# One adaLN transformer block with a routed expert layer on one core: one activation table for logarithm and exponential, the second norm in steps of a block, and four operations placed elsewhere

## The chip, the core and the metric

The kernel runs on one core of one Trainium2 chip. The core has a matrix engine, TensorE (PE in the profile; its weight loads are listed as PEld), and three engines for elementwise work: VectorE (DVE), ScalarE (ACT) and GpSimd (POOL). SyncE (SP) issues most of the transfers (DMA), POOL the gathers and scatters. Each engine works through its own queue in the order in which the program was written, and waits for the others by semaphores. PE multiplies from the on-chip memory SBUF and writes its products into eight banks of PSUM, which the other engines read out.

The metric is the time of one execution on the device in microseconds (us), and lower is better. All arithmetic is in float32.

## The reference

x holds 4 batches of 512 tokens with 512 features. A conditioning vector c makes six rows of modulation a batch. The block is, cut to what matters:

```python
mod = (silu(c) @ wmod).reshape(4, 6, 1, 512)
sa, ca, ga, sb, cb, gb = mod[:, 0], ..., mod[:, 5]      # ga, gb kept away from zero
h = layernorm(x) * (1 + ca) + sa
x = x + ga * attention(h)        # 16 heads of 128, causal softmax, Wq Wk Wv Wo with biases
h = layernorm(x) * (1 + cb) + sb
x = x + gb * ffn(h)
# ffn: softmax router over 8 experts, the best 2 of them a token (silu(h Wg) * (h Wu)) Wd
#      of width 352, weighted and summed, plus a shared expert of width 704
# layernorm: (x - mean) / sqrt(var + 1e-5), over the 512 features
```

## The kernel before

**Products by seven.** Every large product is cut into 2 by 2 blocks and made with seven block products in place of eight (`seven`, L515). The operands therefore carry seven slots: four blocks as they are, and sums of them, made by `sums_of_a` (L490) and `sums_of_b` (L497) into slots 4, 5 and 6 and, in place, into slot 2 or 1. `PROD` (L487) says which two slots each product takes. PE makes them in the order 1, 2, 6, 7, 5, 4, 3: the first two take the blocks as loaded (slots 0, and 1 with 2), the third takes slot 5 of both sides, the fourth slots 2 and 4, the fifth slots 4 and 1, the sixth 3 and 6, the seventh 6 and 3. A product lies in a PSUM bank of the tag "w", of which there are three, until DVE or ACT has read it out. `most_of_b` (L504) and `rest_of_b` (L510) are `sums_of_b` in two pieces: slots 4, 5 and 6 first, without touching slot 1, and then slot 1 in place.

**Opening (L869 to L884, L1061 to L1073).** SP loads c, the modulation weights wm for SA, x of batch 0, wm for CA, the biases, and then the weights wk, wq and wv, whose sums POOL makes as they land. `normed` (L211) takes the first norm: for each of the four blocks of 128 tokens, statistics on DVE (L227, L228), then rstd as exp(-0.5 ln(var + eps)) with Ln and Exp on ACT (L233, L234), then the scaling on DVE (L244). `modulate` (L166) makes one row set of modulation on PE. `quadrants` (L878) turns the normed x by PE transposes (`turned_block`, L267; `turn`, L275), applies the modulation and makes the sums.

**Attention (loop from L1076).** The heads go in 16 groups, G, of four heads, u; four groups a batch. For each head, `scores` (L782 to L800) makes four rows of logits, their masked maxima (DVE), Exp (ACT), and the scaling by the reciprocal of the sums (rsum, L797, on DVE, then L800 on ACT). `attend` (L803) transposes the weights on PE (L810), copies them out as probT (L818 on DVE, L820 on ACT) and multiplies with v (po, L824). `weave_at` writes the steps of these generators into the queues by hand: after each step of attention so many steps of the next projections (`fill`), and at the positions in `spots` one step of a side generator. The side generators are the first norm and the turning of the next batch, and `second_norm` (L949) of the batch before: `normed` with n = 2, which also multiplies by ga, adds x (L221, L222), and applies rows cb and sb (L261 on DVE, L262 on POOL), and then the router (`route`, L293), whose first step transposes the normed blocks. `fine` lists the blocks after which `normed` ends a step; its default, (1,), puts two blocks into a step. All queues but POOL's follow the written order exactly.

**Shared expert, first half (L1579 to L1614).** For batches 0 and 1, the turned second-norm outputs h2s are loaded; `tail_products` (L1210) multiplies the last 64 columns of the shared expert, `shared_tail` (L1223) applies Silu, and `sums_of_b` makes the sums of h2s, for batch 0 on POOL and for batch 1 on DVE. `shared(0)` (PE lines L1241 and L1322) then runs its products, while `slots_found` does the second norm and the routing of batch 3 beside it (here the scaling is on ACT, L253, and `idle` is true). The tiles' weights and rows are loaded during the last products.

**Expert tiles (L1616 to L1647).** 36 tiles of 128 routed tokens: `tile_in` (L1452) transposes a tile's rows and copies them to xT, `tile_hidden` makes gate and up (pgt and put, L1468), `tile_down` the result yt, which `keep` stores (L1507). A branch for more than 36 tiles follows (L1649). Pools of SBUF are opened for one phase each (`open_phase`): "tiles" takes the place of "half1", "half2" the place of "tiles", and a tile in the new pool has to wait until the last reader of that place is done.

**Shared expert, second half (from L1659).** The same for batches 2 and 3, with the gathering of the experts' results.

Of the kernel before, what the change touches and what calls it, by code (L numbers as in the profile page):

```python
# [44 lines left out]
EPS = 1e-5  # L45
SA, CA, GA, SB, CB, GB = range(6)
# [3 lines left out]
def adaln_block_kernel(  # L50
# [105 lines left out]
    nc.scalar.activation(cs, cT, AF.Silu)  # L156
# [9 lines left out]
    def modulate(sec, wm):  # L166
        pm = bank("ps", f"pm_{sec}")[:B, :]
        for c in range(NC):
            nc.tensor.matmul(
                pm, lhsT=cs[:, c, :], rhs=wm[:, c, :], start=(c == 0), stop=(c == NC - 1)  # L170
            )
        row = work.tile([B, D], F32, tag="gy", name=f"row_{sec}")
# [12 lines left out]
        if sec in (SA, CA):  # L185
            pt = bank("pt", f"pmt_{sec}")
            for c in range(NC):
                nc.tensor.transpose(
                    pt[:, c * B : (c + 1) * B], row[:, c * P : (c + 1) * P], ident[:B, :B]
                )  # L190
            nc.vector.tensor_copy(
                mod[:, sec].rearrange("p c b -> p (c b)"), pt[:, : NC * B]
            )
        else:
            nc.sync.dma_start(out=mod_rows[sec], in_=row)
# [13 lines left out]


    def normed(b, n, fine=(1,)):  # L211


        if n == 1:
            src = xh = late["first"]
        else:
            src = xres[b]
            xh = late["x"]
            rows = late["mod"]
            for t in range(NTB):  # L220
                nc.vector.tensor_mul(src[:, t, :], src[:, t, :], ga_bc)  # L221
                nc.gpsimd.tensor_add(src[:, t, :], src[:, t, :], xh[:, t, :])  # L222
                yield
        mv = small.tile([P, NTB, 2], F32, tag="mv", name=f"mv_{n}_{b}")
# [7 lines left out]
        nc.vector.tensor_scalar_add(rstd, mv[:, :, 1], EPS)  # L232
        nc.scalar.activation(rstd, rstd, AF.Ln)  # L233
        nc.scalar.activation(rstd, rstd, AF.Exp, scale=-0.5)  # L234
        idle = n == 2 and b == B - 1
# [39 lines left out]
    def turn(b, c, xh, dst):  # L275

        pt = turned_block(b, 1, xh, c)
# [212 lines left out]
    def sums_of_a(eng, w):  # L490

        eng.tensor_add(w[:, 4], w[:, 2], w[:, 3])
        eng.tensor_sub(w[:, 2], w[:, 0], w[:, 2])
        eng.tensor_sub(w[:, 5], w[:, 4], w[:, 0])
        eng.tensor_sub(w[:, 6], w[:, 1], w[:, 5])

    def sums_of_b(eng, w):  # L497

        eng.tensor_sub(w[:, 4], w[:, 3], w[:, 1])
        eng.tensor_sub(w[:, 1], w[:, 1], w[:, 0])  # L500
        eng.tensor_sub(w[:, 5], w[:, 3], w[:, 1])
        eng.tensor_sub(w[:, 6], w[:, 5], w[:, 2])
# [365 lines left out]

    wm = load_wmod(att, "v", SA)  # L869
    load_first(0)  # L870
# [7 lines left out]
    def quadrants(b):  # L878
        h7[b] = att.tile([P, 7, 2, HW], F32, tag="h7", bufs=1, name=f"h7_{b}")
        for c in range(NC):  # L880
            turn(b, c, late["first"], h7[b])
# [67 lines left out]
    def second_norm(b):  # L949
        yield from normed(b, 2)  # L950
# [71 lines left out]
    def drain(gen):  # L1022
        for _ in gen:
            pass
# [3 lines left out]
    def rest_of_modulation():  # L1028
        secs = (GA, SB, CB, GB)
        wm = load_wmod(work, "xh", secs[0])  # L1030
        for k, sec in enumerate(secs):
            yield
            yield
            modulate(sec, wm)
# [25 lines left out]

    with tc.manual_schedule(engines={ENG.PE, ENG.DVE, ENG.Activation, ENG.SP}):  # L1061
        norm = normed(0, 1)
        drain(steps(norm, 2))
        modulate(SA, wm)
        drain(norm)
        modulate(CA, wm2)
# [3 lines left out]
        drain(quadrants(0))  # L1070
# [6 lines left out]
        for G in range(NGB):  # L1077
# [14 lines left out]
            for u in range(GH):  # L1092
# [8 lines left out]
                if g == 0 and b > 0 and u > 0:  # L1101
                    if u == 1:
                        second = side = second_norm(b - 1)
                    spots = (1, 3, 5, 7)
# [347 lines left out]
    def tile_in(i, xt):  # L1452
# [5 lines left out]
        xT = phase[-1].tile([P, NC, P], F32, tag="xT", name=f"xT_{i}")  # L1458
# [33 lines left out]
    def tile_down(i, hT_t):  # L1492
# [9 lines left out]
        yt = phase[-1].tile([P, D], F32, tag="yt", name=f"yt_{i}")  # L1502
# [59 lines left out]
    with tc.manual_schedule(engines={ENG.PE, ENG.DVE, ENG.Activation, ENG.SP}):  # L1562
# [20 lines left out]
        shared_tail(0, tail_products(0))  # L1583
        sums_of_b(nc.gpsimd, h2s[0])
        shared_tail(1, tail_products(1))
        sums_of_b(nc.vector, h2s[1])
# [26 lines left out]
        xts = {0: load_rows(0), 1: load_rows(1)}  # L1613
        drain(main)  # L1614
# [3 lines left out]
        turned = {0: tile_in(0, xts.pop(0))}  # L1618
# [180 lines left out]
```

## Time and profile before

| what | value |
|---|---|
| three runs | 1780.13, 1779.38 and 1787.22 us, median 1780.13 us |
| the profiled execution | 1783.91 us |
| its span in the profile | 1782.2 us |
| PE busy | 1710.5 us, 96% of the span |
| DVE busy | 898.9 us, 50% |
| ACT busy | 545.6 us, 31% |
| POOL busy | 589.5 us, 33% |
| mean granted clock of PE | 0.99 of full speed |
| activation table loads in the norms (L233, L234) | 16, of 1283 ns each |

How it is read: a row of the waits gives who waited for whom, the total in us, the number of waits and the longest. A row of the timeline gives the start in us, the duration, the engine, the line of the kernel, the operation, what it writes and reads, how many instructions are merged in it, and in brackets how long the engine had been idle and what ended that. A row of a stretch gives its bounds, its length, the busy time of PE, PEld, DVE, ACT and POOL with their instructions, the granted clock, the busy share of the DMA engines and GB/s. Matmuls overlap in a pipeline and their ends are modelled.

### The profile page before, as it was taken

Reading aid. Unit: us, or ns where it says so; the run is one execution under the profiler, and the core shown is the slowest. Engines: PE = TensorE matmul, PEld = TensorE weight load, DVE = VectorE, ACT = ScalarE, POOL = GpSimd, SP = SyncE. Lnnn points to the kernel's source line nnn. Section 1 sums busy time; section 2 is a strip of 40 time slices with the busy share of each in tenths; the row PEclk is TensorE's granted clock in tenths of the full one; section 3 lists DMA queues with packets and bytes.
Section 4 is the critical chain, followed back from the end, with each engine's and each line's share of the span. In section 5 each row is a group of like instructions: output and inputs, shape, how many; then the busy total and the mean of one; then the engine's idle time right before and its main releaser. Section 6 shows DMA issues by size and latency. Waiting matters only on the chain. (4 is left out here: it accounts for less than half of the span.)

```text
span 1782.2 us, 21702 instructions
## 1 busy us (share of the span) xinstructions
PE 1710.5 (96%) x7550; PEld 1305.8 (73%) x7550; DVE 898.9 (50%) x1892; ACT 545.6 (31%) x1312; POOL 589.5 (33%) x702
## 2 busy tenths in 40 slices
PE   6999999999999999899999989999899999999998
PEld 4767787786777888688788867787687656555687
DVE  4554454546546455654655465444666122111298
ACT  1024444304454421444541154444220111111120
POOL 6334653314354220525331255533520021000360
PEclk9999999999899999999999999999999999999999
DMA  6569989736343254334224275616224554565352
GB/s 243 176 209 298 291 283 308 232 113 228 94 165 112 80 166 145 122 101 147 104 100 148 95 243 185 196 53 238 111 74 181 200 202 166 176 221 200 105 180 70
DMA packets 158526, 301.14 MB, mean 169 GB/s; under 512 B 19136, under 2 KB 99008, under 8 KB 151760
## 3 DMA queue, kind: packets, MB, share of 16 engines
q1 hardware_dynamic: 153296, 282.96, 47.4%
q0 software_dynamic: 5120, 16.78, 2.8%
q8 instruction: 61, 1.00, 0.2%
q14 instruction: 49, 0.40, 0.1%
HBM read 247.25 MB, written 97.03 MB: 193 GB/s over the span
## 5 line engine op out<-in xcount | busy, mean ns | idle before, releaser
L793 ACT ACTIVATE prob<-ps,nmax 128x128 f32<-128x128 f32 (+3 forms) x256 | 134.2, 525 | 362.0 <-DVE nmax L791 354.3
L645 PE MATMUL w_k<-h,wk 128*128 128x256 f32 x896 | 224.1, 388 | 3.9 <-ACT p_k L657 2.1
L693 PE MATMUL w_v<-wv,h 128*128 128x256 f32 x896 | 206.1, 379 | 3.0 <-DVE kT L660 1.8
L730 PE MATMUL w_o<-wo,oS 128*128 128x256 f32 x896 | 208.9, 379 | 0.0
L607 PE MATMUL w_q<-h,wq 128*128 128x256 f32 x896 | 203.6, 382 | 1.8 <-DVE qT L633 1.8
L607 PEld LDWEIGHTS w_q<-h,wq 128*128 128x128 f32 x896 | 169.9, 191 | 28.2 <-issue 2.6
L645 PEld LDWEIGHTS w_k<-h,wk 128*128 128x128 f32 x896 | 166.5, 196 | 26.4 <-ACT p_k L657 5.1
L693 PEld LDWEIGHTS w_v<-wv,h 128*128 128x128 f32 x896 | 167.3, 190 | 24.9 <-DVE kT L660 2.2
L730 PEld LDWEIGHTS w_o<-wo,oS 128*128 128x128 f32 x896 | 164.6, 190 | 21.3 <-issue 1.4
L782 PE MATMUL ps<-kT,qT 128*128 128x128 f32 (+3 forms) x512 | 174.0, 441 | 1.6 <-ACT prob L793 1.4
L824 PE MATMUL po<-probT,v 128*128 128x512 f32 (+3 forms) x512 | 151.3, 435 | 12.7 <-DVE probT L818 12.6
L824 PEld LDWEIGHTS po<-probT,v 128*128 128x128 f32 x512 | 94.9, 190 | 70.5 <-issue 29.8
L810 PEld LDWEIGHTS ppt<-ident,prob 128*128 128x128 f32 x640 | 83.3, 142 | 82.5 <-issue 36.2
L800 ACT ACTIVATE prob<-prob,rsum 128x128 f32<-128x128 f32 (+3 forms) x256 | 122.8, 551 | 63.8 <-DVE rsum L797 63.8
L1241 PE MATMUL w_s<-h2s,ws 128*128 128x256 f32 x560 | 125.6, 382 | 7.2 <-DVE hid L1227 1.8
L743 POOL TENSOR_TENSOR xres<-xres,p_o 128x512 f32<-128x512 f32 x48 | 61.0, 1271 | 210.4 <-DVE xres L743 118.7
L791 DVE TENSOR_REDUCE nmax<-ps 128x1 f32<-128x128 f32 (+3 forms) x256 | 125.8, 491 | 8.8
L810 PE MATMUL ppt<-ident,prob 128*128 128x128 f32 x640 | 109.8, 279 | 15.0 <-ACT prob L800 12.2
L1241 PEld LDWEIGHTS w_s<-h2s,ws 128*128 128x128 f32 x560 | 104.8, 190 | 26.2 <-issue 3.1
L789 DVE TENSOR_TENSOR ps<-ps,cmask 128x128 f32<-128x128 f32 x256 | 75.1, 293 | 61.4 <-PE ps L782 51.2
L1495 PE MATMUL pyt<-wdn,hTt 128*128 128x512 f32 (+1 forms) x216 | 98.7, 593 | 0.0
L1478 DVE TENSOR_TENSOR ht<-tsg,put 128x352 f32<-128x352 f32 x36 | 18.8, 521 | 150.0 <-PE put L1468 125.5
(286 smaller groups left out, 2370.4 us busy)
## 6 DMA issues: line engine op xcount, KB each, us to landing
wgu<-in_wexp_dram SPq DMA_DIRECT2D x36, 1408.0 KB
xs<-nothing SPq DMA_DIRECT2D x15, 2304.0 KB
wdn<-in_wexp_dram SPq DMA_DIRECT2D x36, 768.0 KB
wo<-sums_o SPq DMA_DIRECT2D x12, 1536.0 KB
wq<-sums_q SPq DMA_DIRECT2D x24, 640.0 KB
wk<-sums_k SPq DMA_DIRECT2D x24, 640.0 KB
wv<-sums_v SPq DMA_DIRECT2D x12, 1280.0 KB
xt<-xs SPq DMA_DIRECT2D x36, 256.0 KB
```

Source lines behind the costliest of these rows:

```text
L607: nc.tensor.matmul(dst, lhsT=w[:, sa, c, :], rhs=h7[b][:, sb_, c, :], start=c == 0, stop=c == 1,)
L645: nc.tensor.matmul(dst, lhsT=w[:, sa, c, :], rhs=h7[b][:, sb_, c, :], start=c == 0, stop=c == 1,)
L693: nc.tensor.matmul(dst[:, t2 * HW : (t2 + 1) * HW], lhsT=h7[b][:, sb_, c, t2 * P : (t2 + 1) * P], rhs=w[:, sa, c, :], start=t2 == 0 and c ...
L730: nc.tensor.matmul(dst[:, t2 * HW : (t2 + 1) * HW], lhsT=oSs[hp][:, sa, t2 * P : (t2 + 1) * P], rhs=w[:, hp, sb_, :], start=t2 == 0 and hp ...
L782: nc.tensor.matmul(ps[:, :n], lhsT=qT[:, q0 : q0 + P], rhs=kT[:, u % 2, :n], start=True, stop=True,)
L791: nc.vector.tensor_reduce(nmax, ps[:, :n], AX.X, ALU.max, negate=True)
L793: nc.scalar.activation(blk, ps[:, :n], AF.Exp, bias=nmax, accum_out=rsum[:, i : i + 1])
L800: nc.scalar.mul(blk, blk, rsum[:, k : k + 1])
L810: nc.tensor.transpose(pt[:, at : at + P], prob[:, QO[i] + j * P : QO[i] + (j + 1) * P], ident,)
L824: nc.tensor.matmul(po[:, j * P :], lhsT=v()[:, j, u * DH : (u + 1) * DH], rhs=probT[:, KO[j] : KO[j] + (NTB - j) * P], start=(j == 0), sto ...
L1241: nc.tensor.matmul(dst[:, n * HW : (n + 1) * HW], lhsT=ws[k][:, sa, c, :], rhs=h2s[b + n][:, sb_, c, :], start=(n == 0 and c == 0), stop=( ...
L1495: nc.tensor.matmul(py, lhsT=hT_t[:fn, k, :], rhs=wdn[i % 2][:fn, k * D : (k + 1) * D], start=(k == 0), stop=(k == len(FCH) - 1),)
```

## The change

- **One table.** `load_lnexp` writes a load of activation table set 6, which holds both Ln and Exp, into ACT's queue: once after the Silu of c at the start, and once ahead of Ln in the second norm of batch 3, which follows Silu. The compiler then places no load of its own for Ln and Exp. The Silu of c moves to the start of the ordered part.
- **Second norm a block a step.** `second_norm` calls `normed` with `fine` = (0, 1, 2), and the head u = 2 of the first group calls the side generator at all eight positions in place of four.
- **Opening.** x is loaded ahead of the modulation weights. The modulation's two products come ahead of the norm's scaling in PE's queue, and the first two turned blocks ahead of the small transposes of the modulation, which now use a bank of the tag "w" in place of "pt".
- **Order of sums.** `sums_of_a` and `sums_of_b` make slot 5 second; `sums_of_b` makes it from slot 4 and slot 0 and no longer from the changed slot 1.
- **Sums of h2s.** In the first half of the shared expert `most_of_b` stands ahead of the tail products (batch 0 on POOL, batch 1 on DVE), and `rest_of_b` for both stands on POOL behind them.
- **First tile's turn.** `tile_in(0)` is called ahead of the last two products of the shared expert's first half, and xT of this tile lies in a place of its own.
- **Last result.** yt of the last tile lies in a part of the gate and up weights that is no longer read, in place of the "tiles" pool.

In the built program the matmuls are the same on PE, ACT has 7 table loads in place of 21, and DVE one instruction less (four sums of h2s of batch 1 become three); POOL and SP have as many as before. On DVE, in each second norm of batches 0 to 2, the first block's statistics stand ahead of the copy of probT (L818) and the readout kT (L660), u_k (L660) behind the third block's statistics, and the first block's scaling and product (L244, L261) ahead of the last copy of probT of that head.

```diff
+LNEXP = 6
...
-    nc.scalar.activation(cs, cT, AF.Silu)
...
-            pt = bank("pt", f"pmt_{sec}")
+            pt = bank("w", f"pmt_{sec}")
...
+    def load_lnexp():
+
+        nc.scalar.add_instruction(
+            mybir.InstLoadActFuncSet(
+                act_func_set_id=LNEXP,
+                name=nc.get_next_instruction_name(),
+                engine=ENG.Activation,
+            )
+        )
...
+        idle = n == 2 and b == B - 1
...
+        if idle:
+            load_lnexp()
         nc.scalar.activation(rstd, rstd, AF.Ln)
         nc.scalar.activation(rstd, rstd, AF.Exp, scale=-0.5)
...
     def sums_of_a(eng, w):
 
         eng.tensor_add(w[:, 4], w[:, 2], w[:, 3])
+        eng.tensor_sub(w[:, 5], w[:, 4], w[:, 0])
         eng.tensor_sub(w[:, 2], w[:, 0], w[:, 2])
-        eng.tensor_sub(w[:, 5], w[:, 4], w[:, 0])
         eng.tensor_sub(w[:, 6], w[:, 1], w[:, 5])
 
     def sums_of_b(eng, w):
 
         eng.tensor_sub(w[:, 4], w[:, 3], w[:, 1])
+        eng.tensor_add(w[:, 5], w[:, 4], w[:, 0])
         eng.tensor_sub(w[:, 1], w[:, 1], w[:, 0])
-        eng.tensor_sub(w[:, 5], w[:, 3], w[:, 1])
         eng.tensor_sub(w[:, 6], w[:, 5], w[:, 2])
...
+    load_first(0)
     wm = load_wmod(att, "v", SA)
-    load_first(0)
     wm2 = load_wmod(att, "wo", CA)
...
-        yield from normed(b, 2)
+        yield from normed(b, 2, (0, 1, 2))
...
+        nc.scalar.activation(cs, cT, AF.Silu)
+        load_lnexp()
         norm = normed(0, 1)
-        drain(steps(norm, 2))
-        modulate(SA, wm)
+        pms = {SA: modulation(SA, wm), CA: modulation(CA, wm2)}
         drain(norm)
-        modulate(CA, wm2)
+        turned = [turned_block(0, 1, late[0], c) for c in range(2)]
+        for sec in (SA, CA):
+            modulate(sec, pms[sec])
...
-        drain(quadrants(0))
+        drain(quadrants(0, turned))
...
-                    spots = (1, 3, 5, 7)
+                    spots = range(8) if u == 2 else (1, 3, 5, 7)
...
-        xT = phase[-1].tile([P, NC, P], F32, tag="xT", name=f"xT_{i}")
+        if i == 0:
+            xT = moe.tile([P, NC, P], F32, tag="xT0", bufs=1, name="xT_0")
+        else:
+            xT = phase[-1].tile([P, NC, P], F32, tag="xT", name=f"xT_{i}")
...
-        yt = phase[-1].tile([P, D], F32, tag="yt", name=f"yt_{i}")
+        if i == NA - 1:
+            yt = wgu[i % 2][:, 2 * S : 2 * S + D]
+        else:
+            yt = phase[-1].tile([P, D], F32, tag="yt", name=f"yt_{i}")
...
-        shared_tail(0, tail_products(0))
-        sums_of_b(nc.gpsimd, h2s[0])
-        shared_tail(1, tail_products(1))
-        sums_of_b(nc.vector, h2s[1])
+        most_of_b(nc.gpsimd, h2s[0])
+        most_of_b(nc.vector, h2s[1])
+        tails = [tail_products(b) for b in range(half)]
+        for b in range(half):
+            shared_tail(b, tails[b])
+            rest_of_b(nc.gpsimd, h2s[b])
...
+        for _ in range(SEVEN - 2):
+            next(main)
+        turned = {0: tile_in(0, xts.pop(0))}
         drain(main)
...
-        turned = {0: tile_in(0, xts.pop(0))}
```

More of the change, by code (lines that the diff above doesn't have):

```diff
@@ L164, in load_wmod, with modulation @@
         return wm
-    def modulate(sec, wm):
+    def modulation(sec, wm):
         pm = bank("ps", f"pm_{sec}")[:B, :]
@@ L171, in modulate @@
             )
+        return pm
+    def modulate(sec, pm):
         row = work.tile([B, D], F32, tag="gy", name=f"row_{sec}")
@@ L232, in normed @@
         nc.vector.tensor_scalar_add(rstd, mv[:, :, 1], EPS)
+        if idle:
+            load_lnexp()
         nc.scalar.activation(rstd, rstd, AF.Ln)
         nc.scalar.activation(rstd, rstd, AF.Exp, scale=-0.5)
-        idle = n == 2 and b == B - 1
         if idle:
@@ L273, in turned_block, with turn @@
         return pt
-    def turn(b, c, xh, dst):
-        pt = turned_block(b, 1, xh, c)
+    def turn(b, c, xh, dst, pt=None):
+        pt = turned_block(b, 1, xh, c) if pt is None else pt
         kh, c2 = divmod(c, 2)
@@ L876, in adaln_block_kernel, with quadrants @@
     wv_t = [load_wv(0, 0)]
-    def quadrants(b):
+    def quadrants(b, turned=()):
         h7[b] = att.tile([P, 7, 2, HW], F32, tag="h7", bufs=1, name=f"h7_{b}")
         for c in range(NC):
-            turn(b, c, late["first"], h7[b])
+            turn(b, c, late["first"], h7[b], turned[c] if c < len(turned) else None)
             if c == NC - 1:
@@ L1033, in rest_of_modulation @@
             yield
-            modulate(sec, wm)
+            modulate(sec, modulation(sec, wm))
             if k + 1 < len(secs):
```

## The prediction

> **What bounds the kernel now.** I read the page first, then the list of what TensorE (PE) waited for over the whole run, then stretches of 10 us for the granted clock, then the timeline at each place where PE stood still. One profiled execution took 1783.9 us, with a span of 1782.2; the other 1.7 us lie around it. The median of the three runs is 1780.1, so this execution is 3.8 us above it. I add up savings on the profiled execution and take them from the median.
>
> ```profile
> span 1782.2 us, 21702 instructions
> PE 1710.5 (96%) x7550; PEld 1305.8 (73%) x7550; DVE 898.9 (50%) x1892; ACT 545.6 (31%) x1312; POOL 589.5 (33%) x702
> ```
>
> PE is busy 96% of the span, so a change that leaves its matmuls alone can win only the idle 72 us and the time that matmuls lose to a lowered clock. The waits of PE name the idle places that this change touches:
>
> ```profile
> PE po L824 <- DVE probT L818: 12.6, 8, 3.0
> PE ppt L810 <- ACT prob L800: 12.2, 17, 2.1
> ...
> PE pgt L1468 <- DVE xT L1459: 2.4, 1, 2.4
> ```
>
> (What waited and for whom; total us, times, longest.) The first two rows are largest in the second norms of batches 0, 1 and 2, and the clock drops there. In the stretches (the third figure from the end is the granted clock; ahead of it the busy us of PE, weight loads, DVE, ACT and POOL):
>
> ```profile
> 440.00:450.00 10.00, 6.72 (x23) 4.27 (x22) 9.79 (x15) 4.58 (x14) 7.16 (x7) 0.72 0.17 44
> 450.00:460.00 10.00, 10.00 (x47) 7.61 (x46) 3.30 (x10) 4.63 (x12) 3.49 (x5) 0.77 0.82 216
> ```
>
> Taken microsecond by microsecond the clock there is either 1.00 or 0.50: half for (0.28+0.23) x 10 x 2 = 10.2 us after batch 0's norm, and by the same sum 6.8 after batches 1 and 2. The norm's step in the timeline:
>
> ```profile
> 438.22 1.28 ACT L234 ACT_TABLE_LOAD   x1
> 438.59 0.55 DVE L818 COPY probT<-ppt 128x384 f32<-128x384 f32 x1
> 439.20 0.92 PE L824 MATMUL po<-probT,v 128*128 128x256 f32 x4 [1.54 <-DVE probT L818]
> ...
> 439.75 0.55 DVE L244 TENSOR_SCALAR xh<-xres,mv,rstd 128x512 f32<-128x512 f32 x1 [0.61 <-ACT rstd L234]
> ...
> 443.48 0.17 DVE L797 RECIPROCAL rsum<-rsum 128x4 f32<-128x4 f32 x1
> ...
> 444.14 1.99 PE L810 MATMUL ppt<-ident,prob 128*128 128x128 f32 x4 [2.14 <-ACT prob L800]
> ```
>
> VectorE (DVE) is the limit in this step: statistics, then the blocks' scaling, and between them the small operations of attention that PE waits for. The two table loads add 0.61 us of DVE idle before the first scaling.
>
> **The change part by part.**
>
> *Table loads.* The build has 7 in place of 21; at 1.28 us each, 18 us leave ScalarE (ACT), which is 31% busy. The loads in the first norms of batches 1 to 3 I cost at nothing: at 253.2 and 254.7 us PE goes on with the attention and w_o products and shows no idle row until 271.8 us, where DVE is late. If that cover were gone it would be 1.3 us a load at most.
>
> *Second norm, batches 0 to 2.* The order changes on DVE: the first block's statistics (0.81 us, from 433.13 to 433.94) go ahead of the earlier probT copy and u_k falls one statistics later; the first block's scaling and product move ahead of the probT copy that PE's po waits for. I redo the step from these rows. DVE was idle 0.60 us before 431.44 (waiting for ppt), and the first block's statistics fill it, ending at 431.65. Later rows come 0.81 us earlier: rstd at 436.77 and nmax until 437.78. Ln and Exp (0.20 us each) without loads are done at 437.4, so the 0.61 us is gone. Then the scaling 0.58 and product 0.61, and probT at 438.97 in place of 438.59: PE's first gap grows by 0.4, from 1.54 to 1.92 us. After it the second block takes what it took (2.54 us to rsum), so rsum comes at 442.09 in place of 443.48. PE's second gap shrinks from 2.14 to 0.4. What follows (the last block's addition on POOL, which PE's transpose of the normed block waits for, at 449.28) moves by the same 1.39 us, because DVE and POOL set it. So 1.4 us a norm, 4.2 for three. The lower end is 0 a norm (PE's first gap grows and the half clock eats the rest), the upper the whole loss. From the first gap's start to the next po takes 20.0, 19.5 and 19.2 us (437.66 to 457.67 and so on) for 12.9 us of matmuls at full clock, so 6.6 us a norm.
>
> *The clock.* Half clock began at 444.28, 748.22 and 1048.38 us: these are 89 and 177 steps of 3.41 us apart, and it lasts 3, 2 and 2 such steps. Going back from 444.28 by steps, those in which PE worked 51% or more (437.45 to 440.87; 270.22 to 273.63, with the 2.99 us gap) were not followed by it, those with 40% or less were (a transpose counted as 0.11 us). With the change, the 5 us around the transposes of prob and of the normed block still hold only some 1.6 us of matmuls. So I keep half clock after each norm and credit only 1 us in all, for the third step after batch 0. The ends are 0 and 7 us (23.8 us at half clock, PE busy some 85%, is 10 lost; about 3 would come back as waiting for POOL's last block).
>
> [...]
>
> *Shared expert's start.*
>
> ```profile
> 1266.01 8.04 PE L1241 MATMUL w_s<-h2s,ws 128*128 128x256 f32 x36 [1.43 <-DVE h2s L501]
> ...
> 1280.17 1.28 ACT L234 ACT_TABLE_LOAD   x1
> ...
> 1282.51 1.99 PE L1241 MATMUL w_s<-h2s,ws 128*128 128x256 f32 x8 [1.09 <-DVE wgu L1253]
> ```
>
> The four h2s sums on DVE (1262.35 to 1266.60) become three, placed where DVE stood idle for 4.78 us before 1258.91. That takes out PE's 1.43, and lets the DVE chain of last norm and products, solid from 1266.60 to 1279.9, begin 4.3 us earlier. The Exp load goes (1.28), for which DVE waited 1.79 us; the loads left lie ahead of rstd and behind it. PE idles here 1.43+0.23+1.09+1.18+0.55 = 4.48 us. One or two gaps stay in small, where DVE waits for ACT's Silu load and four scalings: I take 4.0, between 1.4 (only the first gap goes) and 4.5. The fourth sum goes to POOL behind the tail products (ended 1260.3) and ahead of the norm's additions there. Four sums end at 1264.7 there (1.27 to 1.59 each) and the fifth near 1266; the product that reads it is due at 1267.0.
>
> *First tile's turn.* PE's 2.40 us before pgt go. The transposes (0.6) now stand ahead of two products, at 1366.2 in place of 1371.3, and wait for the rows' transfer, issued at 1354.5; the DMA engines are quiet by 1361. Ahead of the products' evacuation the copy (0.61) delays DVE, but pgt's bank is that of the product before, free at 1369.1. So 2.4, with 0 as the end where pgt finds another wait.
>
> *Last result.* At 1676.95 POOL's memset and at 1676.96 DVE's L1227 start together, after the branch that ACT left at 1675.44. Both write where the last result lay until its transfer had read it. Elsewhere, DVE follows ACT's Silu at 1676.1: 0.9 of PE's 1.84 us goes (ends 0 and 1.5).
>
> *Opening.* The row below decides:
>
> ```profile
> 33.45 0.72 POOL L664 TENSOR_TENSOR u_k<-u_k,u_k 128x256 f32<-128x256 f32 x1
> ...
> 34.68 1.99 PE L693 MATMUL w_v<-wv,h 128*128 128x256 f32 x8 [1.81 <-DVE kT L660]
> ```
>
> POOL makes 20 sums without a pause from 14.35 us, when the first wk has landed, to 33.45; PE waits for what comes behind them. SP sends the same bytes ahead of wk, so 14.35 stays. x lands near 6.7 in place of 9.85, wm near 9.85; PE's modulation products (5.7 us cold, then 3.4) end near 18.9, and the first turns come within a microsecond of before. The h sums in the new order let the third product start 1.1 us earlier, which the wait at 34.68 eats. What counts: DVE's scaling (15.14 to 18.76) no longer slows POOL's sums (0.91 beside 0.72), some 0.5 us. Ends: -0.5 (turns late) and 1.5.
>
> *Sum.* 0.5 + 4.2 + 1.0 + 4.0 + 2.4 + 0.9 = 13.0 us: 1783.9 becomes 1770.9, and from the median 1767.
>
> **The rivals.** (1) The norms give nothing, because the probT copy behind the first block's scaling costs PE as much as the second gap returns, or the first gap of 1.92 us now falls into one 3.41 us step and starts the half clock earlier. 13.0-5.2 = 7.8 us remain: 1772, within 0.5%. For it speaks that PE is at the edge in the first gap (51% and 55% worked); against it that DVE's chain is shorter by 1.4 us whatever PE does. (2) PE stays above the edge and the clock stays full: 13+7 = 20 us, 1760. For it: every gap but the last shrinks in sum; against it the 1.6 us of work in 5 us. (3) Slower: half clock starts at the grown first gap and lasts. One more step of 3.41 us costs 1.7 us; with 0.4 of gap and four more steps a norm it is 3 x 7.2 = 22 us against 7.8 gained, 1794. It decides from about 3.1 more steps a norm, (7.8+8.9)/3 = 5.6 us lost beyond now; the longest seen is 3 steps in all. (4) The change doesn't do what it says: the loads would come back before each Ln. The built order has 7 loads, none between the norms of batches 1 to 2, so this is nearly out; it would leave 9 us, 1771.
>
> **How the numbers follow.** Forecast 0.64, rival 1 0.16, rival 2 0.13, rival 3 0.04, rival 4 0.03. About 0.5% (8.9 us) is what a measurement of this kernel can tell from no change. The forecast's own sum falls to 9.0 us if the shared expert gives 1.4 and the opening and the last result nothing (13.0-2.6-0.5-0.9), and reaches 16 if each norm loses one step of half clock less; I give one chance in twenty that it is under 8.9; with rival 2 that makes 0.74 faster; rivals 1 and 4 and the forecast's tail 0.22 same; 0.04 slower. The range runs from rival 2 (1760) to a little above rival 1, where two small parts also fail: 1776.
>
> **What would show it.** In the profile after: 7 table loads; rsum in the second norm 4.4 us after the first gap begins, in place of 5.8; first gap near 1.9, second near 0.4; half clock still seen after the norms; w_s with no wait for h2s and less than 1 us for L1253 and L1266; pgt without its 2.4; L1227 of the second half less than 1 us behind the branch; w_v near 34.2. I am wrong if the first gap reaches 3 us, if half clock is gone (then 1760), or if DVE's chain at the shared expert still holds PE for 3 us.

## The result and the profile after

The changed kernel takes 1762.5 us (median of four runs, 1761.36 to 1764.14) where the kernel before, run beside it, takes 1782.5 us: a ratio of 0.9886 with a 95% interval of 0.9859 to 0.9914, so 20 us faster. The forecast was 1767. The profiled execution took 1764.14 us, with a span of 1762.4; before it was 1783.9 and 1782.2, and the difference of the two spans, 19.8 us, is what the traces have to account for. In this part line numbers are those of the changed kernel (Ln and Exp L249 and L250, the scaling of xh L259, POOL's addition L277, probT L833, rsum L812, po L839, ppt L825, the shared expert's w_s L1259); rows of another run carry the line numbers of its own kernel.

The head of the page:

```profile
span 1762.4 us, 21698 instructions
PE 1701.7 (97%) x7550; PEld 1302.2 (74%) x7550; DVE 896.5 (51%) x1891; ACT 528.5 (30%) x1298; POOL 589.5 (33%) x703
```

PE has the same 7550 matmuls and is busy 8.8 us less (1710.5 before): most of that is clock, as the table of steps below shows. The rest of the 19.8 us is idle time. What PE waited for (total us, times, longest):

```profile
PE po L839 <- DVE probT L833: 12.3, 6, 2.7
PE pm L169 <- DMA wm<-in_wmod_dram: 10.8, 2, 9.7
PE pln L285 <- POOL xh L277: 5.5, 6, 1.6
PE ppt L825 <- ACT prob L815: 5.1, 13, 1.5
PE w_k L660 <- DVE h L515: 2.4, 1, 2.4
...
PE w_s L1259 <- DVE hid L1245: 1.8, 1, 1.8
```

The wait for prob fell from 12.2 to 5.1, the one for probT hardly (12.6 to 12.3), pgt's 2.4 is gone, and the wait for h in the opening grew from 1.8 to 2.4. The second norm of batch 0 in the timeline:

```profile
436.38 0.55 DVE L833 COPY probT<-ppt 128x384 f32<-128x384 f32 x1
436.99 0.92 PE L839 MATMUL po<-probT,v 128*128 128x256 f32 x4 [1.93 <-DVE probT L833]
439.20 0.16 DVE L812 RECIPROCAL rsum<-rsum 128x4 f32<-128x4 f32 x1
439.85 0.73 PE L825 MATMUL ppt<-ident,prob 128*128 128x128 f32 x2 [0.42 <-ACT prob L815]
443.11 0.33 PE L285 MATMUL pln<-ident,xh 128*128 128x128 f32 x1 [0.33 <-POOL xh L277]
445.00 0.33 PE L285 MATMUL pln<-ident,xh 128*128 128x128 f32 x1 [1.56 <-POOL xh L277]
```

PE's first gap begins at 435.06 (436.99 less 1.93). Rsum comes 4.14 us behind that (5.82 before), the second gap is 0.42 in place of 2.14, and the last block's transpose starts 9.94 us behind it (11.62 before). PE now runs ahead of POOL's last block and waits 1.56 us for it. The stretches (third figure from the end: the granted clock):

```profile
440.00:450.00 10.00, 7.58 (x34) 5.41 (x33) 6.91 (x12) 5.29 (x14) 7.83 (x9) 0.83 0.54 129
450.00:460.00 10.00, 10.00 (x60) 8.24 (x60) 4.54 (x14) 5.62 (x14) 0.00 (x0) 1.00 0.56 175
```

Half clock lasts 0.17 x 10 x 2 = 3.4 us here, one step in place of three.

At the start of the shared expert only one of PE's five gaps is left, and the first tile's transposes stand between the products, so pgt follows without a wait:

```profile
1272.59 5.42 PE L1259 MATMUL w_s<-h2s,ws 128*128 128x256 f32 x24 [0.55 <-PE w_s L1259]
...
1348.59 0.60 PE L1473 MATMUL pxt<-ident,xt 128*128 128x128 f32 x4
...
1354.22 2.53 PE L1489 MATMUL pgt<-wgu,xT 128*128 128x352 f32 x8
```

Where the profiled 19.8 us lie, between marks that both traces have (the start of the w_q run at 108.38 and 110.30; the first head's ppt ahead of the shared expert at 1238.61 and 1226.01; pht of the first tile at 1380.03 and 1359.80; the end of the span):

| part | before | after | difference |
|---|---|---|---|
| opening | 108.38 | 110.30 | +1.9 |
| attention, norms, router of three batches | 1130.23 | 1115.71 | -14.5 |
| shared expert's start and first tile | 141.42 | 133.79 | -7.6 |
| tiles and second half | 402.17 | 402.60 | +0.4 |

### The profile page after: what moved, and what is told of

It reads as the page before. It is cut to its first block, busy times and chain, and to the rows that moved or that the text cites. A ratio compares the mean times of both kernels' runs of the same rounds, so it can differ in the third digit from the quotient of the medians.

```text
span 1762.4 us, 21698 instructions
## 1 busy us (share of the span) xinstructions
PE 1701.7 (97%) x7550; PEld 1302.2 (74%) x7550; DVE 896.5 (51%) x1891; ACT 528.5 (30%) x1298; POOL 589.5 (33%) x703
## 5 line engine op out<-in xcount | busy, mean ns | idle before, releaser
L660 PE MATMUL w_k<-h,wk 128*128 128x256 f32 x896 | 223.5, 387 | 4.6 <-DVE h L515 2.4
L660 PEld LDWEIGHTS w_k<-h,wk 128*128 128x128 f32 x896 | 165.9, 195 | 27.9 <-ACT p_k L672 5.3
L839 PE MATMUL po<-probT,v 128*128 128x512 f32 (+3 forms) x512 | 150.4, 435 | 12.3 <-DVE probT L833 12.3
L839 PEld LDWEIGHTS po<-probT,v 128*128 128x128 f32 x512 | 95.5, 190 | 68.7 <-issue 30.3
L825 PEld LDWEIGHTS ppt<-ident,prob 128*128 128x128 f32 x640 | 83.3, 143 | 73.4 <-issue 34.7
L1259 PE MATMUL w_s<-h2s,ws 128*128 128x256 f32 x560 | 124.4, 381 | 3.3 <-DVE hid L1245 1.8
L1259 PEld LDWEIGHTS w_s<-h2s,ws 128*128 128x128 f32 x560 | 105.0, 190 | 20.8 <-issue 2.7
L825 PE MATMUL ppt<-ident,prob 128*128 128x128 f32 x640 | 108.4, 278 | 7.6 <-ACT prob L815 5.1
```

The source lines that it names most:

```text
L660: nc.tensor.matmul(dst, lhsT=w[:, sa, c, :], rhs=h7[b][:, sb_, c, :], start=c == 0, stop=c == 1,)
L825: nc.tensor.transpose(pt[:, at : at + P], prob[:, QO[i] + j * P : QO[i] + (j + 1) * P], ident,)
L839: nc.tensor.matmul(po[:, j * P :], lhsT=v()[:, j, u * DH : (u + 1) * DH], rhs=probT[:, KO[j] : KO[j] + (NTB - j) * P], start=(j == 0), sto ...
L1259: nc.tensor.matmul(dst[:, n * HW : (n + 1) * HW], lhsT=ws[k][:, sa, c, :], rhs=h2s[b + n][:, sb_, c, :], start=(n == 0 and c == 0), stop=( ...
```

## The experiments

**One table alone.** The kernel before with `load_lnexp` and its two calls, nothing else.

```diff
+        if n == 2 and b == B - 1:
+            load_lnexp()
         nc.scalar.activation(rstd, rstd, AF.Ln)
...
+        nc.scalar.activation(cs, cT, AF.Silu)
+        load_lnexp()
         norm = normed(0, 1)
```

> The kernel before with the one table alone (7 loads in place of 21), nothing else of the change. Theory A (DVE's chain sets the second norms, the loads cost PE only where DVE waits for Exp): per norm the 0.61 us of DVE idle goes and nothing else, so PE's first gap stays 1.54 and the second falls to 1.5; in the shared expert the 1.28 us Exp load goes. 3 x 0.6 + 1.3 = 3.1 us, time 1779 against 1782.5. Theory B (the 18 us of loads on ACT were felt all over attention and kept the clock low): more than 8 us, time below 1774.

It took 1778.12 us, a ratio of 0.9978 (0.9966 to 0.999): 4 us, with 1.8 and 6.1 as the ends of the interval. The gaps of the first norm:

```profile
440.81 0.92 PE L836 MATMUL po<-probT,v 128*128 128x256 f32 x4 [1.53 <-DVE probT L830]
445.06 0.73 PE L822 MATMUL ppt<-ident,prob 128*128 128x128 f32 x2 [1.80 <-ACT prob L812]
```

The loads' 0.61 us come off DVE's wait, but of the second gap only 0.34 go. At the shared expert the wait of 1.09 us for L1253 is gone; the others stay. Theory A holds against B, though the interval is too wide to tell its 3.1 us from 4. One gap shrank that neither the forecast nor Theory A had counted, PE's wait for probT behind the first norm of batch 1. Before, in this run, and in the changed kernel:

```profile
271.80 0.89 PE L824 MATMUL po<-probT,v 128*128 128x256 f32 x4 [2.99 <-DVE probT L818]
273.44 0.78 PE L836 MATMUL po<-probT,v 128*128 128x256 f32 x3 [2.19 <-DVE probT L830]
271.49 0.89 PE L839 MATMUL po<-probT,v 128*128 128x256 f32 x4 [2.09 <-DVE probT L833]
```

It is 2.98 us in the next run, which has all loads, and 2.03 to 2.38 in every kernel with one table.

**A block a step alone.** The kernel before with `fine` and the eight positions, and all loads still there.

```diff
-        yield from normed(b, 2)
+        yield from normed(b, 2, (0, 1, 2))
...
-                    spots = (1, 3, 5, 7)
+                    spots = range(8) if u == 2 else (1, 3, 5, 7)
```

> The kernel before with the second norm in steps of a block and the eight positions alone, both loads still in each norm. Theory A: the first block's scaling now stands ahead of the probT copy and has to wait for Exp behind two loads, ready near 1.3 us later than the scaling could start; PE's first gap grows from 1.54 to about 2.9 us, the second shrinks to about 1. Nothing is won: 0 to 1 us a norm, time 1781 to 1783; the two edits gain together what neither gains alone. Theory B (the order of DVE is what counts, the loads are aside): 1.4 us a norm here too, 1778.

1778.95 us, 0.998 (0.9968 to 0.9993): 3.3 us. Its first norm:

```profile
440.16 1.64 PE L824 MATMUL po<-probT,v 128*128 128x256 f32 x4 [3.09 <-DVE probT L818]
446.06 0.33 PE L270 MATMUL pln<-ident,xh 128*128 128x128 f32 x1 [0.26 <-POOL xh L262]
447.95 0.33 PE L270 MATMUL pln<-ident,xh 128*128 128x128 f32 x1 [1.56 <-POOL xh L262]
```

The first gap grew as A said, because the block's scaling, now ahead of probT in DVE's queue, waits for rstd behind two loads; the gain is B's all the same. The second gap is gone, and this profile has 17 us of half clock between the first two marks, where the kernel before has 30.7. With one table and a block a step together the first gap is 1.9 in place of 3.1. These two parts alone, without the rest of the change, were not run together, and the new order of sums was never run by itself; so what the two give beyond 4 and 3.3 us is read from the changed kernel's trace alone.

**The opening of before.** The changed kernel with x loaded behind the first modulation weights, the modulation and the turns in the old order, one table kept.

```diff
-    load_first(0)
     wm = load_wmod(att, "v", SA)
+    load_first(0)
...
-        pms = {SA: modulation(SA, wm), CA: modulation(CA, wm2)}
-        drain(norm)
-        turned = [turned_block(0, 1, late[0], c) for c in range(2)]
-        for sec in (SA, CA):
-            modulate(sec, pms[sec])
+        drain(steps(norm, 2))
+        modulate(SA, modulation(SA, wm))
+        drain(norm)
+        modulate(CA, modulation(CA, wm2))
```

> The changed kernel with the opening of before (modulation weights ahead of x, products and turns in the old order), the table and the new order of sums kept. Theory A (the new opening is a loss: the second row of modulation waits on DVE behind the first one's copy, the h sums then fall beside POOL's large sums and PE drops to half clock): the projection of q starts 1.5 to 2.5 us earlier than in the changed kernel (38.0), near 36, and the whole is 1760.5 against 1762.5. Theory B (what was lost in the opening is lost to half clock by the chance of where its steps fall): start between 37 and 38.

1763.98 us, 0.9901 (0.988 to 0.9921), with w_q's run at 36.63 us, between the two theories, and the mark at 109.39 us: undoing the opening brings 0.9 of the 1.9 us back in the profiled execution, and none in the time. The same opening with the call of POOL's sums of the first wv moved behind the first key projection:

```diff
-    wv_t = [load_wv(0, 0)]
+    wv_t = [wts.tile([P, 7, 2, 2 * DH], F32, tag="wv", bufs=1, name="wv_0_0")]
+    nc.sync.dma_start(
+        out=wv_t[0].rearrange("p q c n -> p (q c n)")[:, : 16 * DH], in_=wv[0]
+    )
...
         drain(next_k(0, 0))
+        sums_of_a(nc.gpsimd, wv_t[0])
```

> As the run before, and the sums of the first wv are written behind the first key projection, their transfer staying where it was, so that POOL reaches the addition u_k earlier. Theory A (POOL's 20 sums hold PE in the opening until 34 us): q starts another 1 to 3 us earlier, near 34, time 1759. Rival (PE is held by DVE's sums of h or by half clock): no further change, 1760.5.

1761.6 us, 0.9881 (0.9861 to 0.9901), w_q's run at 35.47 and not near 34, the mark at 107.70, no half clock in the opening. On POOL two of the four sums still ran ahead of u_k, since POOL's queue is not written by hand. PE's waits for kT, first in the run before, then here:

```profile
34.36 2.48 PE L708 MATMUL w_v<-wv,h 128*128 128x256 f32 x8 [2.67 <-DVE kT L675]
...
31.66 1.99 PE L708 MATMUL w_v<-wv,h 128*128 128x256 f32 x8 [0.93 <-DVE kT L675]
35.47 5.45 PE L622 MATMUL w_q<-h,wq 128*128 128x256 f32 x24 [1.82 <-DVE kT L675]
```

u_k begins on POOL at 30.42 us in place of 33.13, and w_v follows it: POOL's sums do hold PE at this place. But the two sums left bring a wait of 1.82 us behind it, so 2.67 us of waiting became 2.75, and the 1.7 us by which the mark is earlier are what the missing step of half clock is worth. That the sums cost time in the opening isn't shown. Then the same move of the wv sums in the new opening:

> The changed kernel with its new opening, but POOL's four sums of the first wv (1.27 us each alone, 1.27 to 1.71 beside DVE's) stand behind the first key projection's work instead of ahead of it. Theory A (what holds PE in the new opening is that these sums run beside DVE's four h sums and slow both, 1.39 to 1.75 us an h sum in place of 0.85 to 1.10): the h sums take 1.1 us or less each, PE's wait w_k <- DVE h of 2.44 us falls to about 1.2, the run of w_q that starts at 38.01 us starts near 35.5, and the mark at 110.30 us comes near 107.7. Theory B (the late turns hold PE, because the row of CA stands behind the copy of the mod of SA on DVE): the turns stay at 22.4 us and the mark moves by less than 1 us.

1765.72 us in one execution. The edit did nothing: POOL ran the four sums at 25.86 to 32.1 us, ahead of u_k, as in the changed kernel, and the mark came at 110.15. So this run decides neither theory, but it repeats the changed opening, and so do all other kernels below that leave it alone. Their marks:

| kernel | mark, us | half clock in the opening |
|---|---|---|
| before; one table; a block a step (old opening) | 108.38; 108.53; 108.59 | 3.4 us each |
| changed; late wv sums (no effect) | 110.30; 110.15 | 3.4 us each |
| extra transposes; both extras; no branch; old h2s sums; no branch and old place of yt | 108.65; 108.32; 109.01; 108.47; 108.54 | 3.4 us each |

From seven executions of one opening: 108.3 to 110.3, median 108.65, against 108.4 to 108.6 in the three of the old one above. So the 1.9 us of the profiled pair are mostly spread between executions. Where the one step of half clock falls doesn't explain it. In the run with the late sums it fell on the first key products, which took 3.22 us; in the changed kernel these took 1.89 and the next ones were slowed, and yet their marks agree:

```profile
24.82 3.22 PE L660 MATMUL w_k<-h,wk 128*128 128x256 f32 x8
29.49 1.97 PE L660 MATMUL w_k<-h,wk 128*128 128x256 f32 x8 [1.45 <-DVE h L515]
```

With the old h2s sums the step began at 24.34 us, with the late sums at 24.09, and the marks are 1.7 us apart. One part of the spread shows in the rows: the sixteen modulation products start 0.85 us apart at first and 0.43 us later, and the change of pace comes at another time in each execution (between 10.9 and 11.4 us before, between 14.8 and 15.5 in the changed kernel), so the same products took 9.83 us in the changed kernel, 8.89 with the late sums and 8.41 with both extras. What makes the rest was not found.

Last of the opening, both rows of modulation taken ahead of their small transposes (with the same move of the wv sums, which again came ahead of u_k):

```diff
-        for sec in (SA, CA):
-            modulate(sec, pms[sec])
+        rows = {sec: row_of(sec, pms[sec]) for sec in (SA, CA)}
+        for sec in (SA, CA):
+            turn_row(sec, rows[sec])
```

> As the kernel with the late wv sums, and on DVE the row of CA is taken from its products ahead of the copy of the mod of SA, so that the row's 0.67 us lie in DVE's wait of 4.11 us for the transposes and PE's wait of 0.85 us for the row goes. Theory A (contention alone): less than 0.5 us earlier than the late wv sums alone, since the turns only meet a later wait. Theory B (the turns count too): the first turn by ACT (L298) starts near 21.5 us in place of 22.39, and the mark that was at 110.30 us is 0.7 to 1.2 us earlier than with the late wv sums alone, near 106.7.

ACT's first turn starts 1.9 us behind the modulation products (19.69 to 21.55) where it was 2.9 (18.96 to 21.83) with the late sums alone, as B said, and the mark is 107.93, the lowest of the new openings. But this execution has no half clock in the opening, which is worth 1.7 us by itself, so how much the rows are worth stays open. The whole, 1766.3 us in one execution, is no faster.

**Work for PE in the gaps.** Twelve extra transposes ahead of the last block's, and then with four extra po products as well.

```diff
         for t in range(NTB):
+            if n == 2 and b < B - 1 and c == 0 and t == NTB - 1:
+                for _ in range(12):
+                    nc.tensor.transpose(pt[:, :P], xh[:, 0, :P], ident)
             nc.tensor.transpose(
```

> The changed kernel with twelve extra transposes of a block that is already normed, written to the same bank and overwritten at once, in the second norms of batches 0 to 2, placed where PE waits 1.56 us for POOL's last block (pln <- POOL xh). They add 12 x 0.11 = 1.3 us of work inside that wait; the result is the same. Theory A (the clock is halved for a step of 3.41 us after one in which PE worked less than about half, and transposes count as work): the half-clock steps behind that wait go, one each after the norms of batches 0 and 1 and one of two after batch 2. Each costs 3.41/2 = 1.7 us, so 5 us in all: 1757.5, with 1760 if part of it comes back as waiting. The 5-us stretches at 445 and 735 us show 1.00 in place of 0.66. Theory B (transposes don't keep the clock up, or the halving doesn't hang on work): the clock drops as before, the added work shows where the half clock has begun, 1762 to 1765.

1763.46 us, 0.9894 (0.9877 to 0.991): no gain. The gap of 1.56 fell to 0.26 and no half clock follows it. But none follows it either in the kernel without the branch and with the old place of yt, where the gap is 1.56 and no work was added, so the transposes alone show nothing for the clock. The steps at 735 and from 1030 us, which lie behind the first gap and not behind this one as I had put it, stay, and the profile has steps at 140, 210 and 435 to 445 us that the changed kernel's lacks.

```diff
         po = bank("po", f"po_{name}")
+        G = int(name.split("_")[0])
+        if G % NG == 0 and G > 0 and u == 1:
+            for _ in range(4):
+                nc.tensor.matmul(
+                    po, lhsT=v()[:, 0, u * DH : (u + 1) * DH],
+                    rhs=probT[:, :S], start=True, stop=True,
+                )
```

> As the kernel with extra transposes, and four extra po products (0.92 us, overwritten by the real ones) ahead of the first po of the second norm, where PE waits 1.9 to 2.7 us for probT. Theory A: the half clock of batch 2 that begins at 1030 us, behind the first gap, goes as well: 1.7 us more than the extra transposes alone, about 1756, and every 5-us stretch around the three norms shows 1.00. But the extra products read probT too, so they start only when it is there and can't fill the gap itself: they lengthen the step by 0.9 us each where PE is then the limit. If that is what decides, this run is 1 to 3 us slower than the one with transposes alone. Theory B: 1765.

1760.56 us, 0.9883 (0.9866 to 0.9899), 1757.3 us of span in the profile, which shows no half clock from 30 us to the end of the batches (440 to 450, 735 to 740, 1030 to 1040):

```profile
440.00:450.00 10.00, 9.42 (x60) 7.26 (x59) 6.65 (x16) 4.08 (x12) 6.45 (x8) 1.00 0.66 178
735.00:740.00 5.00, 4.39 (x28) 3.50 (x28) 4.86 (x8) 2.72 (x6) 3.74 (x3) 1.00 0.15 48
1030.00:1040.00 10.00, 8.79 (x52) 6.57 (x50) 8.92 (x15) 4.82 (x13) 8.04 (x8) 1.00 0.79 272
```

The last kernel below has both extras too and no half clock around its norms either: six norms without a step, where the eleven kernels without extra work have 3 to 7 steps there. So here work that is overwritten counted for the clock; which of the two extras does it was not separated. My price for the products was wrong: the rows of 128x512 on their line took 3.60 us in the first norm (from 431.37), not 0.92, did not wait for probT, as I had expected them to, and covered the first gap whole.

**What the stretch of the three batches is made of.** For every run: PE's idle rows between the first two marks added up, and the half clock from the 5-us stretches, (1 - clock) x 10 each. The half clock comes in steps of 3.41 us (30.7 / 9). Four products of w_k that took 1.03 us ahead of a step took 2.07 in one (the last kernel, at 210.80 and 212.37 us, granted clock 0.50), so a step is counted as a loss of half its length.

| kernel | length | idle | half clock (steps) | length - idle - half clock / 2 |
|---|---|---|---|---|
| before | 1130.2 | 32.9 | 30.7 (9) | 1082.0 |
| one table alone | 1128.0 | 32.9 | 27.2 (8) | 1081.5 |
| a block a step alone | 1125.3 | 34.6 | 17.0 (5) | 1082.2 |
| changed | 1115.7 | 27.5 | 13.7 (4) | 1081.4 |
| opening of before | 1117.3 | 27.9 | 17.0 (5) | 1080.9 |
| the same, wv sums moved | 1115.8 | 27.4 | 13.7 (4) | 1081.6 |
| no branch | 1115.7 | 26.5 | 17.0 (5) | 1080.7 |
| old h2s sums | 1119.3 | 29.9 | 13.6 (4) | 1082.5 |
| late wv sums | 1118.3 | 27.2 | 20.6 (6) | 1080.7 |
| rows first | 1121.5 | 29.8 | 20.5 (6) | 1081.4 |
| no branch, old yt | 1117.9 | 27.2 | 20.6 (6) | 1080.4 |
| extra transposes | 1118.0 | 24.6 | 17.1 (5) | 1084.8 |
| both extras | 1114.3 | 18.4 | 0 | 1096.0 |
| old opening, wv sums moved, both extras (last below) | 1118.4 | 17.8 | 10.2 (3) | 1095.5 |

The last column is the same within 2.1 us in the eleven kernels without extra work, while the length varies by 14.5. Around the norms alone there are 7 steps before, 5 with one table, 4 with a block a step, and 3 or 4 in the eight kernels that have both and no extra work. Which of the rest appear, at 140, 210, 270 or 340 us, differs between kernels whose work there is the same: 1 to 3 in ten of the eleven, and none in the changed one.

Each row is one execution. The granted clock that is listed for every execution says what is usual: the mean of (1 - clock) x span is 16.1 us in 34 executions of the kernel before, 15.5 in ten with one table alone, 13.5 in ten with a block a step alone, and 10.6 in four of the changed kernel, whose clocks run from 0.992 to 0.996. So some 5.5 of the 20 us are clock, where the profiled pair has 8.5; a block a step alone brings about half of that, and one table alone hardly any.

Both extras buy 6.8 us of clock and 9.1 of idle time with 14.6 us of work, a net 1.4.

**The sums of h2s as before.**

```diff
-        most_of_b(nc.gpsimd, h2s[0])
-        most_of_b(nc.vector, h2s[1])
-        tails = [tail_products(b) for b in range(half)]
-        for b in range(half):
-            shared_tail(b, tails[b])
-            rest_of_b(nc.gpsimd, h2s[b])
+        shared_tail(0, tail_products(0))
+        sums_of_b(nc.gpsimd, h2s[0])
+        shared_tail(1, tail_products(1))
+        sums_of_b(nc.vector, h2s[1])
```

> The changed kernel with the sums of h2s placed as in the kernel before (POOL's behind the first batch's tail products, DVE's behind the second's, instead of the greater part ahead of both). Theory A (the placement is worth the 1.43 us wait of w_s and the 4.3 us that DVE's solid chain starts earlier; the table load only 1.1): PE's wait w_s <- DVE h2s of 1.4 us is back, and PE's idle time at the shared expert's start is 2.5 to 3.5 us in place of 0.55: 1765 to 1766. Theory B (the table load is the greater part, because it lies in the chain of the last norm): under 1.5 us of idle time there, 1763 to 1763.5.

```profile
1254.41 8.19 PE L1259 MATMUL w_s<-h2s,ws 128*128 128x256 f32 x36 [0.69 <-DVE h2s L515]
1263.14 8.95 PE L1259 MATMUL w_s<-h2s,ws 128*128 128x256 f32 x40 [0.54 <-PE w_s L1259]
1273.28 3.90 PE L1259 MATMUL w_s<-h2s,ws 128*128 128x256 f32 x16 [1.18 <-DVE wgu L1284]
1277.72 2.61 PE L1259 MATMUL w_s<-h2s,ws 128*128 128x256 f32 x11 [0.54 <-PE w_s L1259]
```

1767.76 us in one execution. Four gaps of 2.95 us in sum are there in place of one of 0.55, and from the second mark to the third it takes 137.19 us in place of 133.79: the placement is worth 3.4 of the 5.0 us won here, as A said. With one table alone this start is 1.3 us shorter than before, which is most of the rest. The wait for the sums is 0.69 and not 1.4, because the sums in their new order make slot 5 second.

**Without the branch.** The block for more than 36 tiles and the load of the count that it tests are left out.

```diff
-            if i == 12:
-                used = nc.values_load(late["used"][0:1, 0:1], min_val=0, max_val=NT)
...
-        with tc.If(used > NA):
...
```

> The changed kernel without the branch for more than 36 tiles: the block that the branch would run, and the load of the count that it tests, are left out (with these inputs it isn't taken; for others the result would lack tiles). Theory A (PE's 1.84 us at the second half's start, the term that I put at 0.9 for the last result's transfer and that gave 0, is the branch itself, on which ACT, POOL, DVE and SP all start together): the gap falls below 0.5 us and the time by 1.5 to 2.4 us, to about 1760.5. Theory B (a transfer still holds it, or the frees behind it): the gap stays within 0.4 us of 1.84, 1762 to 1763.

First the changed kernel at the branch, then this one:

```profile
1655.03 1.99 PE L1259 MATMUL w_s<-h2s,ws 128*128 128x256 f32 x8 [0.72 <-ACTq L1677]
...
1657.17 0.59 ACT L1283 COPY wgu<-w_s 128x512 f32<-128x512 f32 x1 [0.28 <-SPq L1677]
1657.31 1.80 POOL L1222 MEMSET hid<- 32x2048 f32 x1 [5.95 <-SPq L1677]
1657.32 2.11 DVE L1245 TENSOR_TENSOR hid<-wgu,pst 32x512 f32<-32x512 f32 x3 [12.00 <-SPq L1677]
1657.43 0.33 SPq L1594 DMA_DIRECT2D xr<-xr  x1
```

```profile
1652.11 1.89 PE L1259 MATMUL w_s<-h2s,ws 128*128 128x256 f32 x8
1652.39 1.80 POOL L1222 MEMSET hid<- 32x2048 f32 x1 [3.06 <-PE pyt L1516]
1653.60 2.81 DVE L1245 TENSOR_TENSOR hid<-wgu,pst 32x512 f32<-32x512 f32 x4 [10.31 <-ACT wgu L1242]
```

ACT, POOL, DVE and SP start within 0.3 us of each other behind the branch, whatever each was waiting for; without it POOL's memset starts 0.3 us behind the products and not 2.3. PE's 0.72 and 1.84 become 0.68, 1.9 us less, within A's 1.5 to 2.4. From the first tile's pht to the end it takes 399.1 us in place of 402.6 (1759.33 in all, one execution). But the twelve profiled executions with the branch, whose work there is the same, take 400.9 to 402.6, so single executions tell no more than 1.8 to 3.5 us. With yt in its old place as well:

```diff
-        if i == NA - 1:
-            yt = wgu[i % 2][:, 2 * S : 2 * S + D]
-        else:
-            yt = phase[-1].tile([P, D], F32, tag="yt", name=f"yt_{i}")
+        yt = phase[-1].tile([P, D], F32, tag="yt", name=f"yt_{i}")
```

> The changed kernel without the branch for more than 36 tiles (its block and the load of the count are left out, as in the kernel without the branch) and with the last result placed as in the kernel before, in the tiles' own buffers. Theory A (behind the branch the transfer of that result is hidden, and it would show once the branch is gone): the memset of hid waits for the transfer of ys, some 2 us behind the copy, and PE has a gap of 1 us or more ahead of the second half's products, about 1 us slower than without the branch alone. Theory B (the place never matters): the second half starts as without the branch alone, with PE's gap of 0.68 us.

```profile
1653.70 1.89 PE L1259 MATMUL w_s<-h2s,ws 128*128 128x256 f32 x8
...
1656.94 1.80 POOL L1222 MEMSET hid<- 32x2048 f32 x1 [6.02 <-DMA ys<-yt]
1656.95 1.39 DVE L1245 TENSOR_TENSOR hid<-wgu,pst 32x512 f32<-32x512 f32 x2 [12.07 <-DMA ys<-yt]
```

Now the memset does wait for the transfer, 3.2 us behind the products. PE loses 0.23 us more by that, not the 1 us that A put there, and the end comes 1.1 us later in one execution (400.15 us from pht), no more than executions differ by. So the transfer was a real wait that lay under the branch.

**Together.** The old opening with the moved wv sums, and both extras, by the diffs above.

> The kernel with the opening of before and its wv sums emitted later, and with the extra transposes and the extra po products in the second norms. Theory A (the two gains add, because the one lies before 110 us and the other at 440 to 1040 us): the mark of the opening at 107.7 us as with that opening alone, no half clock around the three norms, about 1759, some 3 us below the changed kernel. Theory B (where the half clock falls is decided anew in each execution, and the sides of a few us that single profiles showed are that): within 1 us of the kernel with extra transposes and products alone (1760.6), and half clock may show at other places (140, 210, 340 us).

1761.35 us, 0.9875 (0.9856 to 0.9893): Theory B. The opening's mark is 107.26 and there is no half clock around the norms, but three steps at 210 and 335 us, and 1118.4 us between the marks. No kernel that does all the work is faster than the changed one by more than the intervals.

## Why the prediction was right, and where it was not

The forecast's mechanism held, and the sum of 13.0 us came out 6.8 short of the profiled 19.8. The 1762.5 us lie nearer to rival 2's 1760 than to the forecast's 1767, but rival 2's condition, a clock that stays full, did not come. Step by step:

- **Table loads.** Seven, as said: behind the load at 2.90 us Ln and Exp of the first norm run at 10.46 and 10.69 without another, so rival 4 is out. Costing the first norms' loads at nothing was not quite right: behind the first norm of batch 1 they cost PE 0.9 us, the gap that was 2.99 and is 2.09. The gaps of 0.38 and 0.63 us at 565.64 and 880.04, a batch later each, are gone too, but eight other kernels without those loads have a gap of 0.38 at one or both of these places, so they can't be put down to the loads.
- **Second norm, 4.2.** Right. From the first gap's start to the last block's transpose: 11.62, 11.62 and 11.62 us before, 9.94, 9.93 and 10.49 after, 4.5 in sum; rsum at 4.14 where I said 4.4; first gaps 1.93, 1.92 and 2.69 where I said 1.92; second 0.42 where I said 0.4. The wait for POOL's last block grew, as its move by the chain's share implied.
- **The clock, 1.0.** The term that was mis-sized. Half clock is still seen after each norm, but in 1, 1 and 2 steps, not 3, 2 and 2, and the two steps at 212 and 338 us, which I had not looked at, are absent: five fewer, 5 x 1.7 = 8.5 us. Of these the two outside the norms (3.4 us) are not the change's but luck; other runs with the same work there show them. Over all executions the clock's share is some 5.5 us. I had reasoned that some 1.6 us of matmuls in 5 us were still too little, and did not ask how many steps the same work would need. Rival 1 is out by the norms' 4.5; rival 2 (full clock throughout) did not come, and rival 3's longer half clock neither.
- **Shared expert's start, 4.0.** 5.0, above the upper end of 4.5. Four of the five gaps went, 3.9 of the 4.48 us, as the 4.0 said; the other 1.0 us lies outside the waits that the rows show. 3.4 us came by the sums, in one execution.
- **First tile, 2.4.** 2.67; pgt found no other wait.
- **Last result, 0.9.** Wrong. The gap is 1.84 as before. I read two engines starting together as a wait for one transfer; four start together, and it is the branch.
- **Opening, 0.5.** The sign in the profiled pair was wrong (+1.9), and over seven executions it is about 0. What I missed is in DVE's order: the row of CA stands behind the copy of the mod of SA, so the turns come later, and the h sums then fall beside POOL's larger wv sums and take 1.39 to 1.75 us each in place of 0.85 to 1.10. What that costs was not separated.

Half clock is seen here without a long gap of PE: between the first two marks PE's longest gap is 2.99 us before and 2.69 in the changed kernel, and half clock comes there in 9 and in 4 steps.

How far the sums of DVE and POOL hold each other up in the changed kernel's opening can be read from its rows: DVE's sums of h start at 25.93, 27.36, 28.91 and 30.58 us and POOL's sums of wv at 25.50, 26.86, 28.41 and 30.07, in turn, a pair every 1.4 to 1.7 us. A sum of 128x512 took 0.69 us on DVE with POOL idle (before, at 1265.27) and 1.27 on POOL with no sum on DVE (before, at 30.87). One after the other these would be 1.96, so here they do not shut each other out for their whole length.

## What to carry to other kernels

Where the matrix engine is 96% busy, take its idle rows and half its half-clock time from the length of a stretch: here what is left is the same to 2 us in eleven kernels, and it shows what an edit bought and what one execution happened to have. An edit that shortens a chain of small operations beside the matrix engine was worth its own length here (4.5 us in three norms) and, on top, steps of half clock: around the norms there were 7 before and 3 or 4 in the kernels with both edits of the norm. When several engines start at the same moment behind a branch, price the branch before any transfer: here it was 1.9 us of PE's waiting for the one and 0.23 for the other.

## What was not expected of the hardware

Half clock comes in whole steps: 30.7, 27.2, 20.6, 17.0, 13.7 and 10.2 us in the runs are 9, 8, 6, 5, 4 and 3 times 3.41, within 0.2 us. Work whose result is overwritten removed it around the norms: in one execution, 60 more matmuls made the batches 1.4 us shorter. A branch that is not taken cost PE 1.9 us of waiting, with four engines idle until they started together; what in the branch holds them was not tried.
